# A block-sparse, LoRA-gated layer: the first LoRA factors of batch 1 loaded into the scratch buffer, and the last block product in two column halves

## Chip, core and metric

The kernel runs on one core of one Trainium2 chip. The metric is device time in microseconds (us), the median of several runs; lower is better. The kernel has five instruction streams: TensorE (PE, matmuls; its weight loads are shown as PEld), VectorE (DVE), ScalarE (ACT), GpSimd (POOL) and SyncE (SP), which does nothing here but issue DMAs. ACT and POOL issue some DMAs too.

## What is computed

```
xn = layernorm(x)                              # x: 2 batches x 1024 x 1024, over the last axis
W  = weight where its 32x32 block of mask is non-zero, else 0
s  = xn @ W.T + bias
coeffs = softmax((mean over tokens of xn) @ Wq.T @ keys.T / sqrt(128))     # 8 experts, per batch
g  = silu(xn @ W_org.T + sum_e coeffs[e] * (xn @ down[e]) @ up[e])
out = x + s * g
```

All data is fp32. There are 8 experts of rank 64, so all LoRA factors together have rank 512: with the softmax coefficients multiplied into the up factors, the gate's weight for one batch is `W_org.T + down @ (c * up)`, 1024 x 1024.

## The kernel before

Every large product is a split one: each operand is kept as a rounded high part and a low remainder, and three matmuls (high x high, high x low, low x high) are accumulated in PSUM. So TensorE does three 128x128 by 128x512 matmuls for each pair of tiles. A high part is written by ScalarE (a copy), the low part by VectorE (a subtraction).

The order of the work on TensorE, VectorE, ScalarE and GpSimd is written by hand (`manual_schedule`, L617): these engines do their instructions in the order in which the code makes them. SP is not among them. A scheduler that simulates the kernel puts SP's DMA issues in order; a DMA then waits in SP's queue until its buffer is free, and everything behind it waits too.

The stages, in order:

- Batch 0 is done as plain products, 8 token tiles by 2 column halves for s and for the gate. Each of these tiles is a `gemm` (L431): 8 contraction tiles `kt`, three matmuls each (L425 to L427), with a weight held in a "slot" of 8 tiles, high and low. `phase` (L496) runs 8 such tiles; behind each it runs some `jobs` that prepare what comes next.
- In the phase of the gate's second half (`jobs_c`, L948), job i loads and masks tile i of the weight of the s product's second half: `s_mul` (L270) loads a 128x512 tile `ws` into staging, VectorE multiplies it by the mask (L274), ScalarE writes the high part into the slot (L277), and `s_lo` writes the low part (L282). Jobs 1 to 5 also prepare sums of batch 1's inputs, which are stored to DRAM (`xv`) from GpSimd's queue (L487).
- Jobs 6 and 7 compute batch 1's softmax coefficients. `steps[1]` (`query`) multiplies the summed inputs by the query weights `wq_sb` on VectorE (L321), `steps[2]` (`scores`) runs in the middle of the last tile of the phase, and `steps[3]` (`soft`) ends in four coefficients per partition (L352).
- Then `scale_up(1, 0)` (L359) makes the scaled up factors of batch 1's first column half: four tiles of 128x512, each loaded by SP (L364), scaled and rounded by ScalarE (L367, the tile `cut`), its low part made by VectorE (L368). Behind it stands job 7's `s_mul`, in the same hand-written order.
- Next come 8 tiles of batch 0's s product (`s_tile`, L1007), with 16 `fold`s (L969) between them. Each fold loads a tile of down (`ds`) and of W_org (`wo`), splits down (`dhi`, L380, and `dlo`, L381), multiplies it by the four `cut` tiles (12 matmuls, L389 to L391), adds W_org (L396), and stores the folded weight to DRAM. Fold 7 makes the second column half's factors, `scale_up(1, 1, homes)`. Some folds are followed by a `fill` (L990), which loads a tile of `xv` into scratch (L1000) and splits it (L1001, L1002).
- Batch 1 is done with a scheme of seven block products in place of eight. There are 8 units, s and gate in turn; `quad` (L1157) does one, a 2 x 2 arrangement of output blocks 128x512, numbered (i, t) here. It runs 7 `product`s (L1143) of 12 matmuls each into three PSUM banks: `pa`, `pb` and `py`. `out_tile` (L1108) finishes a block. In the first unit of a pair it keeps a gate tile. In the second it multiplies (L1124 for s: PSUM plus bias, times the kept tile), adds the residual x and stores to `out` (L1134). In the last unit the residual comes from a tile loaded by `res_load` (L1136), three buffers of which are used in turn, and VectorE adds it (L1133).

Buffers that matter: the staging pool `stage` has 6 buffers of 128x512 (tag `st`), shared by `ws`, the `us` tiles of `scale_up`, `ds`, `wo` and the sums' tile `xt`; a tile takes the buffer that came free first. The scratch tile `misc` (L101) has three parts of 128x512. Part 0 first holds the mask's expansion matrix, parts 1 and 2 the query weights `wq_sb` (L117). Later all three serve the fills and the second `scale_up` as landing places.

The end of the last unit, before, is this:

```python
            nc.scalar.copy(pa, pb)
            nc.vector.tensor_tensor(pb, pb, s5, ALU.add)
            slot(4)
            product(u, 6, 2, py, False)
            out_tile(u, 0, 1, py)
            out_tile(u, 1, 1, pb)
            res_load(u, 1, 0)
            slot(5)
            product(u, 3, 6, pa, False)
            out_tile(u, 1, 0, pa)
```

Of the kernel before, what the change touches and what calls it, by code (L numbers as in the profile page):

```python
# [14 lines left out]
ALU = mybir.AluOpType  # L15
AX = mybir.AxisListType

P = 128
B = 2
S = 1024  # L20
D = 1024
NKT = D // P
NH = 512
NQ = 256
# [8 lines left out]
def kernel(  # L33
# [26 lines left out]
    nc = tc.nc  # L60
# [5 lines left out]
    def close(*cms):  # L66
# [34 lines left out]
    misc = c0pool.tile([P, 3, NH], F32, name="misc")  # L101
# [4 lines left out]
        out=ex4, in_=ex4, compare_op=ALU.is_ge, fill=0.0, base=0,  # L106
# [3 lines left out]
        out=ex4, in_=ex4, compare_op=ALU.is_ge, fill=0.0, base=3,  # L110
# [407 lines left out]
    J = lambda f, *a: (lambda: f(*a))  # L518
# [98 lines left out]
    with tc.manual_schedule(engines={mybir.EngineType.PE, mybir.EngineType.DVE, mybir.EngineType.Activation, mybir.EngineType.Pool}):  # L617
# [330 lines left out]
        def jobs_c(i):  # L948
            if i == 6:
                yield steps[0]  # L950
                yield steps[1]
            if i == 7:
                yield steps[3]
                yield J(scale_up, 1, 0)
            yield J(s_mul, s1, 1, i)
            yield J(s_lo, s1, 1, i)
            if i in (1, 3):
                yield J(wide_load, (i + 3) // 2, 0)
                yield J(wide_load, (i + 3) // 2, 1)
            if i < 6:  # L960
                yield J((wide_a, wide_b)[i % 2], 1 + i // 2)

        split_at[(0, 1, 7)] = steps[2]
        phase("y", 0, 1, y01, False, jobs_c)


# [20 lines left out]
        xw = {}  # L987
# [27 lines left out]
        units = [("s", 0), ("y", 0), ("y", 1), ("s", 1), ("y", 2), ("s", 2), ("y", 3), ("s", 3)]  # L1015
# [88 lines left out]
        gates = {}  # L1104
        held = {}
        pools_b1 = {}

        def out_tile(u, i, t, ps):  # L1108

            kind, p = units[u]  # L1110
            n = p + 4 * i
            bias = bias_t[:, n : n + 1]
            if u % 2 == 0:
                g = pools_b1["gate"].tile([P, NH], F32, name="gate")
                if kind == "s":
                    nc.scalar.activation(g, ps, AF.Identity, bias=bias)
                else:
                    nc.scalar.activation(g, ps, AF.Silu)
                gates[(p, i, t)] = g
                return  # L1120
            g = gates.pop((p, i, t))
            res = held.pop((i, t), None)
            if kind == "s":
                nc.vector.scalar_tensor_tensor(g, ps, bias, g, ALU.add, ALU.mult)  # L1124
            else:
                y = pools_b1["tmp"].tile([P, NH], F32, name="yt", tag="yt", bufs=1)
                nc.scalar.activation(y, ps, AF.Silu)
                nc.vector.tensor_tensor(g, g, y, ALU.mult)  # L1128
            if res is None:
                nc.gpsimd.dma_start(g, xT[n * P : (n + 1) * P, S + t * NH : S + (t + 1) * NH], accum_op=ALU.add)  # L1130
                res = g
            else:
                nc.vector.tensor_tensor(res, res, g, ALU.add)  # L1133
            nc.sync.dma_start(out[S + n * P : S + (n + 1) * P, t * NH : (t + 1) * NH], res)  # L1134

        def res_load(u, i, t):  # L1136
            if u == len(units) - 1:
                n = units[u][1] + 4 * i
                res = pools_b1["tmp"].tile([P, NH], F32, name="rest", tag="rest", bufs=3)
                nc.sync.dma_start(res, xT[n * P : (n + 1) * P, S + t * NH : S + (t + 1) * NH])  # L1140
                held[(i, t)] = res

        def product(u, a, m, ps, start, js=range(4)):  # L1143
            o = ow[u]
            for j in js:
                for k, (wl, xl) in enumerate(((0, 0), (0, 1), (1, 0))):
                    nc.tensor.matmul(  # L1147
                        ps, lhsT=o[:, a, wl, j, :], rhs=xw[j][:, m, xl, :],
                        start=start and j == 0 and k == 0, stop=j == 3 and k == 2, skip_group_check=True,
                    )  # L1150

        def snap(ps, tag):
            t = pools_b1["tmp2"].tile([P, NH], F32, name=tag, tag=tag, bufs=1)
            nc.scalar.copy(t, ps)  # L1154
            return t

        def quad(u, ahead, behind=()):  # L1157

            def after(k):
                for job in behind[k : k + 1]:  # L1160
                    for f in job:
                        f()

            def slot(k):
                for job in ahead[k]:
                    job()

            pa = ps_acc.tile([P, NH], F32, name="acc_ps", tag="acc_ps")
            if u == 0:
                py = ps_s.tile([P, NH], F32, name="py", tag="ps_s")  # L1170
                product(u, 0, 0, pa, True, (0, 1))
                product(u, 4, 3, py, True, (0, 1))
                product(u, 0, 0, pa, True, (2, 3))
            else:
                product(u, 0, 0, pa, True)
            after(0)
            pb = ps_acc.tile([P, NH], F32, name="acc_ps", tag="acc_ps")
            nc.scalar.copy(pb, pa)  # L1178
            slot(0)
            if u == 0:  # L1180
                product(u, 4, 3, py, True, (2, 3))
            else:
                py = ps_s.tile([P, NH], F32, name="py", tag="ps_s")
                product(u, 4, 3, py, True)
            after(1)
            s5 = snap(py, "s5")
            res_load(u, 0, 0)
            slot(1)
            product(u, 5, 4, pb, False)
            after(2)  # L1190
            s2 = snap(pb, "s2")
            nc.vector.tensor_tensor(py, py, s2, ALU.add)  # L1192
            res_load(u, 0, 1)
            slot(2)
            product(u, 1, 1, pa, False)
            after(3)
            out_tile(u, 0, 0, pa)
            res_load(u, 1, 1)
            slot(3)
            product(u, 2, 5, pb, False)  # L1200
            after(4)
            nc.scalar.copy(pa, pb)
            nc.vector.tensor_tensor(pb, pb, s5, ALU.add)
            slot(4)
            product(u, 6, 2, py, False)
            out_tile(u, 0, 1, py)
            out_tile(u, 1, 1, pb)
            res_load(u, 1, 0)
            slot(5)
            product(u, 3, 6, pa, False)  # L1210
            out_tile(u, 1, 0, pa)
            slot(6)
# [10 lines left out]
        behind = [[J(fill, j, m, xs_pool) for j in (2, 3)] for m in ORDER_X[2:]]  # L1223
        behind[1].insert(0, store_late)
        quad(0, ahead, behind)
        close(cm_xs)
        cm_t, pools_b1["tmp"] = open_pool("tmp", 1, side="right")
        for u in range(1, len(units)):
            quad(u, unit_jobs(u + 1))
# [57 lines left out]
```

## Time and profile before

| what | value |
|---|---|
| median of 3 runs (lowest, highest) | 461.75 us (460.07, 463.16) |
| the profiled execution | 462.08 us |
| its span, first to last instruction | 460.1 us |
| mean granted TensorE clock | 0.986 |
| DMA traffic over the span | 89.52 MB, mean 195 GB/s |

TensorE's busy time by stretch of the span, from the table by stretches:

| stretch (us) | PE busy (us) | granted clock | DMA share |
|---|---|---|---|
| 80 to 140 | 60.00 of 60 | 1.00 | 0.73 |
| 140 to 200 | 59.67 of 60 | 1.00 | 0.65 |
| 200 to 209 | 9.00 of 9 | 1.00 | 1.00 |
| 209 to 220 | 8.27 of 11 | 0.69 | 0.79 |
| 220 to 254 | 34.00 of 34 | 1.00 | 0.84 |
| 258 to 298 | 40.00 of 40 | 1.00 | 0.75 |
| 308 to 440 | 132.00 of 132 | 1.00 | 0.42 |
| 440 to 456 | 15.16 of 16 | 1.00 | 0.14 |

How to read it: a row of the profile names the source line, the engine, the operation, what it writes and reads, and its shape; then come times in us. "PE busy" counts an engine with a matmul in flight; at half the granted clock it is busy too, so the clock stands beside it. A timeline row has the start in us, the duration in us, the engine and line, and in square brackets how long the engine had been idle and what released it. "SPq" rows are DMA issues; the time on the row is that of the issue, and landing is told apart.

### The profile page before, as it was taken

How to read it: one execution, taken by the hardware profiler on the slowest of the kernel's cores; microseconds unless marked ns; L12 is line 12 of the kernel's file. 1: busy time of each engine (PE TensorE's matmuls, PEld its weight loads, DVE VectorE, ACT ScalarE, POOL GpSimd, SP SyncE). 2: the span in 40 equal slices, each digit the busy share in tenths (PEclk: the TensorE clock that was granted, in tenths of full speed). 3: DMA queues.
4: the chain of work that ended last, by engine and by line, in shares of the span. 5: the costliest groups of instructions: out<-in, count | busy, mean ns of one | idle time of the engine just before them, and what ended most of it. 6: DMA issues, size and time to landing. Idle time of an engine off the chain costs nothing.

```text
span 460.1 us, 5752 instructions
## 1 busy us (share of the span) xinstructions
PE 444.7 (97%) x2047; PEld 365.4 (79%) x2047; DVE 305.1 (66%) x492; ACT 169.3 (37%) x277; POOL 59.5 (13%) x72
## 2 busy tenths in 40 slices
PE   7799999999999999997999999999999999999995
PEld 5689888888887888885888788877888888888884
DVE  5889778666775788866546776669466294465624
ACT  3576624363323132213324233158243422441510
POOL 3764210000010202230000000000020020002000
PEclk9899999999999999997999999999999999999999
DMA  8995406687862586799778985664274246218003
GB/s 267 390 350 196 146 24 205 183 281 255 287 230 93 186 317 227 277 309 303 243 249 276 297 274 152 207 219 137 79 147 134 85 98 177 91 24 220 31 1 114
DMA packets 47404, 89.52 MB, mean 195 GB/s; under 512 B 4752, under 2 KB 14992, under 8 KB 47376
## 3 DMA queue, kind: packets, MB, share of 16 engines
q1 hardware_dynamic: 32784, 70.28, 46.1%
q0 software_dynamic: 3840, 10.49, 8.9%
q10 hardware_dynamic: 10752, 8.39, 5.7%
q8 instruction: 16, 0.26, 0.2%
q14 instruction: 12, 0.10, 0.1%
HBM read 69.21 MB, written 19.92 MB: 194 GB/s over the span
## 4 chain that ended last, share of the span: by engine, by line
PE 85%; DVE 8%; DMA 4%; issue 1%; ACT 1%; SPq 0%; ACTq 0%; DVEq 0%
PE acc_ps L1147 23%; PE acc_ps L425 11%; PE acc_ps L426 11%; PE acc_ps L427 11%; PE py L1147 9%; PE psw L391 6%; PE psw L389 6%; PE psw L390 6%; DMA ws<-in_wT_dram 2%; DMA raw<-in_x_dram 1%; DVE slot L558 1%; DVE ramp L549 1%; DMA misc<-in_up_dram 1%; DVE st L144 1%; DVE xw L1002 1%
## 5 line engine op out<-in xcount | busy, mean ns | idle before, releaser
L1147 PE MATMUL acc_ps<-xw,ow 128*128 128x512 f32 x480 | 113.6, 393 | 0.4 <-ACT acc_ps L1178 0.4
L425 PE MATMUL acc_ps<-slot,xgrp 128*128 128x512 f32 (+1 forms) x288 | 107.4, 373 | 2.8 <-ACT slot L277 2.7
L426 PE MATMUL acc_ps<-slot,xgrp 128*128 128x512 f32 (+1 forms) x288 | 106.8, 371 | 2.7 <-DVE slot L558 2.7
L427 PE MATMUL acc_ps<-slot,xgrp 128*128 128x512 f32 (+1 forms) x288 | 106.4, 369 | 0.7 <-DVE xgrp L570 0.7
L1147 PEld LDWEIGHTS acc_ps<-xw,ow 128*128 128x128 f32 x480 | 90.0, 188 | 21.3 <-ACT acc_ps L1178 0.8
L426 PEld LDWEIGHTS acc_ps<-slot,xgrp 128*128 128x128 f32 x288 | 54.9, 191 | 12.6 <-DVE slot L558 3.6
L425 PEld LDWEIGHTS acc_ps<-slot,xgrp 128*128 128x128 f32 x288 | 54.8, 190 | 12.3 <-ACT slot L277 3.1
L427 PEld LDWEIGHTS acc_ps<-slot,xgrp 128*128 128x128 f32 x288 | 55.0, 191 | 10.2 <-DVE xgrp L570 1.1
L391 PE MATMUL psw<-cut,dlo 128*128 128x512 f32 x128 | 50.9, 397 | 0.8 <-DVE dlo L381 0.8
L389 PE MATMUL psw<-cut,dhi 128*128 128x512 f32 x128 | 51.0, 399 | 0.0
L390 PE MATMUL psw<-cut,dhi 128*128 128x512 f32 x128 | 50.6, 395 | 0.0
L1147 PE MATMUL py<-xw,ow 128*128 128x512 f32 x192 | 46.9, 392 | 0.0
L1147 PEld LDWEIGHTS py<-xw,ow 128*128 128x128 f32 x192 | 36.1, 188 | 8.1
L1047 DVE TENSOR_TENSOR ow<-raw,ow 128x1024 fp32r<-128x1024 f32 (+1 forms) x32 | 34.5, 1087 | 10.4 <-ACT ow L1046 10.4
L1130 POOL DMA_DIRECT2D gate<-in_xT_dram x12 | 10.5, 906 | 203.0 <-DVE gate L1128 133.9
L380 ACT CAST dhi<-ds 128x512 fp32r<-128x512 f32 x32 | 19.8, 617 | 40.0 <-PE psw L390 23.8
L396 DVE TENSOR_TENSOR wo<-wo,psw 128x512 f32<-128x512 f32 x32 | 22.0, 686 | 18.6 <-PE psw L391 18.5
L1046 ACT CAST ow<-raw 128x1024 fp32r<-128x1024 f32 (+1 forms) x32 | 29.4, 940 | 1.6 <-DVE wo L396 1.6
L391 PEld LDWEIGHTS psw<-cut,dlo 128*128 128x128 f32 x128 | 24.5, 192 | 6.7 <-DVE dlo L381 1.2
L390 PEld LDWEIGHTS psw<-cut,dhi 128*128 128x128 f32 x128 | 24.6, 192 | 5.4
L389 PEld LDWEIGHTS psw<-cut,dhi 128*128 128x128 f32 x128 | 24.6, 192 | 5.2
L1192 DVE TENSOR_TENSOR py<-py,s 128x512 f32<-128x512 f32 x8 | 5.6, 698 | 30.7 <-ACT s L1154 30.7
(160 smaller groups left out, 477.6 us busy)
## 6 DMA issues: line engine op xcount, KB each, us to landing
ds<-in_down_dram SPq DMA_DIRECT2D x32, 256.0 KB, 3.7
wo<-in_worgT_dram SPq DMA_DIRECT2D x32, 256.0 KB, 3.8
raw<-in_x_dram SPq DMA_DIRECT2D x11, 512.0 KB, 6.5
res<-in_x_dram SPq DMA_DIRECT2D x16, 256.0 KB, 3.8
out_dram<-res ACTq DMA_DIRECT2D x16, 256.0 KB, 2.7
raw<-in_wu_dram SPq DMA_DIRECT2D x8, 512.0 KB, 5.1
yu<-wo ACTq DMA_DIRECT2D x16, 256.0 KB, 4.1
xs<-xv SPq DMA_DIRECT2D x16, 256.0 KB, 4.0
```

What stands on the lines that cost most here:

```text
L380: nc.scalar.copy(dhi, ds)
L389: nc.tensor.matmul(ps, lhsT=dhi[:, c, :], rhs=u[c][:, 0, :], start=c == 0, stop=False)
L390: nc.tensor.matmul(ps, lhsT=dhi[:, c, :], rhs=u[c][:, 1, :], start=False, stop=False)
L391: nc.tensor.matmul(ps, lhsT=dlo[:, c, :], rhs=u[c][:, 0, :], start=False, stop=c == 3)
L396: nc.vector.tensor_tensor(ws, ws, ps, ALU.add)
L425: nc.tensor.matmul(ps, lhsT=xs[:, kt, 0, cols], rhs=w[:, kt, 0, wc], start=kt == 0, stop=False)
L426: nc.tensor.matmul(ps, lhsT=xs[:, kt, 0, cols], rhs=w[:, kt, 1, wc], start=False, stop=False)
L427: nc.tensor.matmul(ps, lhsT=xs[:, kt, 1, cols], rhs=w[:, kt, 0, wc], start=False, stop=kt == NKT - 1)
L1046: nc.scalar.copy(o[:, a:b, 0], raw[:, a:b])
L1047: nc.vector.tensor_tensor(o[:, a:b, 1], raw[:, a:b], o[:, a:b, 0].bitcast(F32), ALU.subtract)
L1130: nc.gpsimd.dma_start(g, xT[n * P : (n + 1) * P, S + t * NH : S + (t + 1) * NH], accum_op=ALU.add)
L1147: nc.tensor.matmul(ps, lhsT=o[:, a, wl, j, :], rhs=xw[j][:, m, xl, :], start=start and j == 0 and k == 0, stop=j == 3 and k == 2, skip_gro ...
```

## The change

There are two edits.

The first: `scale_up(1, 0)` gets homes for three of its four tiles, the three parts of `misc`. `scale_up` uses `homes[c]` where there is one, and a staging tile only for c = 3.

The second is in the last unit alone. Block (1, 1) is finished ahead of the product `py`; the residual of block (1, 0) is loaded ahead of it too, in the code; and the last product, into `pa`, is done for columns 0 to 255 and then for columns 256 to 511, each half with its own end and its own store. For this `product` and `out_tile` get a column range.

```diff
@@ jobs_c
             if i == 7:
                 yield steps[3]
-                yield J(scale_up, 1, 0)
+                yield J(scale_up, 1, 0, [misc[:, k, :] for k in range(3)])
             yield J(s_mul, s1, 1, i)
             yield J(s_lo, s1, 1, i)
@@ out_tile
-        def out_tile(u, i, t, ps):
+        def out_tile(u, i, t, ps, cols=None):
...
+            if cols is not None:
+                g, res = gates[(p, i, t)][:, cols], held[(i, t)][:, cols]
+                nc.vector.scalar_tensor_tensor(g, ps[:, cols], bias, g, ALU.add, ALU.mult)
+                nc.vector.tensor_tensor(res, res, g, ALU.add)
+                c0 = t * NH + cols.start
+                nc.sync.dma_start(out[S + n * P : S + (n + 1) * P, c0 : c0 + NQ], res)
+                return
@@ product
-        def product(u, a, m, ps, start, js=range(4)):
+        def product(u, a, m, ps, start, js=range(4), cols=slice(0, NH)):
...
                     nc.tensor.matmul(
-                        ps, lhsT=o[:, a, wl, j, :], rhs=xw[j][:, m, xl, :],
+                        ps[:, cols], lhsT=o[:, a, wl, j, :], rhs=xw[j][:, m, xl, cols],
@@ quad
             slot(4)
+            if u == len(units) - 1:
+                out_tile(u, 1, 1, pb)
+                res_load(u, 1, 0)
+                product(u, 6, 2, py, False)
+                out_tile(u, 0, 1, py)
+                for c in (slice(0, NQ), slice(NQ, NH)):
+                    product(u, 3, 6, pa, False, cols=c)
+                    out_tile(u, 1, 0, pa, c)
+                return
             product(u, 6, 2, py, False)
             out_tile(u, 0, 1, py)
             out_tile(u, 1, 1, pb)
-            res_load(u, 1, 0)
             slot(5)
             product(u, 3, 6, pa, False)
             out_tile(u, 1, 0, pa)
```

## The prediction

> **What bounds the kernel now.** I read the page first, then the chain of waits, then the timeline of SP's queue and the table by stretches around the one place where TensorE stands still, and last the timeline of the end.
>
> ```profile
> span 460.1 us, 5752 instructions
> PE 444.7 (97%) x2047; PEld 365.4 (79%) x2047; DVE 305.1 (66%) x492; ACT 169.3 (37%) x277; POOL 59.5 (13%) x72
> PEclk9899999999999999997999999999999999999999
> ```
>
> TensorE is the bound: 97% busy, so only its gaps, its slow clock and the work behind its last matmul can be won. The clock row has one low digit in mid-kernel, slice 19 (207 to 219 us). The chain of waits, in order of time, says what happens there:
>
> ```profile
> 202.82 8.54 DMA ws<-in_wT_dram
> 211.38 0.70 DVE ws L274
> 212.11 0.63 ACT slot L277
> 212.78 0.80 PE acc_ps L425
> ```
>
> The last tile of the weight for the s half (job 7) is loaded late, takes 8.54 us to land, and then needs VectorE and ScalarE before TensorE may go on. TensorE's previous matmul started at 209.66; with 0.227 us from one 512-column matmul to the next (12 of them take 2.73 us in the chain), it has stood since 209.89. The timeline of SP's queue says why the load is late:
>
> ```profile
> 195.45 0.37 SPq L272 DMA_DIRECT2D ws<-in_wT_dram  x1
> 195.88 1.89 SPq L364 DMA_DIRECT2D us<-in_up_dram  x4
> 199.90 1.55 SPq L1000 DMA_DIRECT2D misc<-xv  x2
> 202.82 0.33 SPq L272 DMA_DIRECT2D ws<-in_wT_dram  x1
> 207.55 0.33 SPq L375 DMA_DIRECT2D ds<-in_down_dram  x1
> ```
>
> Four factor loads take four of the six staging buffers, and the ws load goes out only at 202.82, right after VectorE's last read of the previous ws tile (L282, 202.10 to 202.79): it waits for that buffer. By then the DMA engines are full (share 1.00 from 200 to 209 us), also with five stores to xv.
>
> The table by stretches (its last three columns: granted clock, DMA share, GB/s) prices the stop:
>
> ```profile
> 211.00:212.00 1.00, 0.00 (x0) 0.00 (x0) 0.62 (x1) 0.00 (x0) 0.00 (x0) 1.00 0.85 264
> 212.00:213.00 1.00, 0.22 (x1) 0.22 (x1) 0.32 (x2) 0.89 (x2) 0.00 (x0) 0.56 0.92 295
> 213.00:214.00 1.00, 1.00 (x2) 0.56 (x3) 1.00 (x2) 1.00 (x3) 0.00 (x0) 0.50 0.99 240
> ...
> 254.00:258.00 4.00, 3.22 (x15) 2.33 (x14) 4.00 (x6) 1.86 (x3) 0.00 (x0) 1.00 0.88 297
> ```
>
> About 2.2 us after TensorE stops the clock halves, and matmuls are 0.427 us apart until 219.10. From 209.89 to 219.10 fourteen steps are made, worth 14 x 0.227 = 3.18 us: the place loses 6.03 us. The last row is the only other stop of the middle, 0.8 us around 255, and there the clock stays at 1.00.
>
> **The change, part by part.** (a) *Homes of the factors.* Three of the four up tiles go to the scratch tile misc instead of staging. Nothing is added: four loads, four ScalarE copies (0.72 us), four VectorE operations (0.75 us), as before. Now the ws load needs no buffer that was just used: its staging buffer has been free since about 189 to 194 us (L282 of the earlier ws tiles). It can go out between 196 and 202 and land well before 209.7.
>
> What is late next is the chain that ran beside it. The softmax coefficients are ready at 205.98. VectorE then does:
>
> ```profile
> 206.77 2.92 DVE L368 SCALAR_TENSOR_TENSOR cut<-us,c,cut 128x512 fp32r<-128x512 f32 x4 [0.79 <-ACT cut L367]
> 211.38 0.69 DVE L274 TENSOR_TENSOR ws<-ws,m_sb 128x512 f32<-128x512 f32 x1 [1.69 <-DMA ws<-in_wT_dram]
> ```
>
> These stand ahead of the ws product on VectorE, so that starts at 209.7, not 211.38: 1.69 us sooner, no more. ScalarE's copy follows at 210.4, the first matmul at about 211.1, the second, which needs L282, at 211.8 (213.50 before): 1.7 us. If the clock is kept, the 13 steps from there to 219.10 take 2.95 us instead of 5.60: 2.65 us. Sum: 4.35 us of the 6.03.
>
> Is the clock kept? Row: a stop of 2.9 us halved it after 2.2 us, one of 0.8 us did not; the new stop is 1.2 us and a wait of 0.5 us behind it. The Trainium skill (TensorE: Matmul & The Clock Gate, Part 1 and the table "Why this matters for your kernels") lets the clock be judged in free-running windows of about 3.4 us and tells one to avoid gaps above about 3 us. By that limit the old stop of 2.9 us should hardly have dropped it, and (a) would be worth 1.7 us only; the trace shows that it dropped. I go by the rows: the new stop is nearer to 0.8, so no drop.
>
> (b) *The loads of misc.* The first factor's home (misc 0) was last read by the mask matmuls at 125 us: its load can go any time before 200. The homes of the second and third hold the query weights, read until 199.87 and 200.48 (L321), so those two loads cannot go before 199.9 and 200.5. ScalarE wants them at 206.7 and 207.4. Nearest rows, issue to landing, in this crowd:
>
> ```profile
> us<-in_up_dram SPq DMA_DIRECT2D x4, 256.0 KB, 6.5
> ...
> misc<-xv SPq DMA_DIRECT2D x2, 256.0 KB, 8.6
> ```
>
> With 6.5 us the third lands at 207.0, in time; with the 9.2 us of the second misc load it lands near 210. The 8.6 comes from standing behind four us loads in one queue, at most two of which now stand there, if SP does not put the fold's loads in between. I take 6.5, cost 0, and keep up to +1.2 us for the other end (rival 1).
>
> The three fills that used to fetch xv into misc at 161.6, 199.9 and 201.1 must now follow the factors' reads, at 207.5 to 209, and be there when ScalarE first wants one (220.69, about 216 after the gain). Landing after about 5 us is 214: hidden by the folds' matmuls. Without that cover ScalarE's in-order queue would hold the next dhi copy, which has some 2 us to spare. The fold's own ds and wo loads come earlier or equal (buffers freed by three); cost 0, as they were hidden even at 207.55. SP's order is not written by hand (the other four engines' is), so all its later waits can shift too; the one stop that depends on it, at 255, is worth 0.8 us: -0.8 to some +4 at worst, taken as 0.
>
> (c) *The end.* Before:
>
> ```profile
> 452.28 2.88 PE L1147 MATMUL acc_ps<-xw,ow 128*128 128x512 f32 x12
> 455.26 0.74 DVE L1124 SCALAR_TENSOR_TENSOR gate<-acc_ps,bias_t,gate 128x512 f32<-128x512 f32 x1
> 456.04 0.69 DVE L1133 TENSOR_TENSOR rest<-rest,gate 128x512 f32<-128x512 f32 x1
> ...
> 46.59 0.28 PE L426 MATMUL acc_ps<-slot,xgrp 128*128 128x256 f32 x1
> 46.71 0.28 PE L427 MATMUL acc_ps<-slot,xgrp 128*128 128x256 f32 x1
> ```
>
> VectorE's last operation ends at 456.73 and the store lands 2.0 us after issue. Matmuls of 256 columns are 0.12 us apart, so two halves take 24 x 0.12 = 2.88 for 2.72: +0.16. Block (1,1) moves to 451.1 to 452.55, beside the twelve py matmuls; block (0,1) runs 452.6 to 454.05; the first half's VectorE pair (0.47 and 0.41 us, scaled from 0.415 for a 256-column read of PSUM at L439) starts at 454.07. If the second half's matmuls run on meanwhile, they end at 455.4 and VectorE is done at 456.3: 0.45 sooner, and the store of half the bytes saves 0.34 more (half of 0.67 us of data at 390 GB/s): -0.8. Against this speaks a rule of the Trainium skill (PSUM — Partial Sum Buffer, "PSUM bank collisions raise a hardware error"): TensorE must not write a bank while VectorE reads it, other columns of it included, so accesses are to be guarded by bank. Both halves lie in one bank of 512 fp32. Then the second half starts when the first half's read ends, at 454.55, takes 12 x 0.12 and 0.3 to drain, VectorE ends at 457.15: 0.42 later, less 0.34: +0.1. No row of the trace shows such a pair. I take +0.1 by the rule, and keep -0.8. The earlier load of (1,0) costs nothing: SP issues it at 450.57 already, when its buffer comes free, and it lands at 453.6.
>
> Sum: -4.35 + 0.1 = -4.25 us. The profiled execution took 462.08 us (span 460.1 and 2.0 around it), 0.3 above the median of 461.75; from the median I forecast 457.5.
>
> **The rivals.** *Rival 1, slower: the scratch loads become the wait.* If SP sends us, ws, ds and wo first, the two bound loads stand where the two misc loads stood and land at 207.9 and 210.3. ScalarE and VectorE then finish the fourth factor at 212.5, the ws product starts at 212.6 and TensorE resumes near 214: about 1.2 us worse than now, clock lost as before, 463.0. It decides by when the third factor lands: each us past 207.4 costs one, and from 209.1 on the change loses (landing + 2.3 = 211.4). For it: the DMA share of 1.00 from 200 to 209 and the 8.6 row. Against: two fewer loads need stand ahead.
>
> *Rival 2: the clock drops all the same.* The stop shortens but the window still counts as idle; then some 15 matmuls run at half speed: 3.4 us lost, gain 1 us, about 460.8. The 0.8 us row speaks against it.
>
> *Rival 3: SP's new order hurts later,* at the second set of factors (240 to 256 us), where SP already waits 4.3 us for a buffer behind VectorE's factor operation. Some 4 us of stop and a lost clock (2.65) against the 4.25 gained: +2.4, 464; with the first place not won either, up to 468.
>
> **How the numbers follow.** A measurement of this kernel tells about 1%, 4.6 us, from no change: below 457.1 is faster, above 466.4 slower. My forecast: 0.58, own range 455.6 to 458.8; its centre is 0.4 us short of the 1% line, and the stop at 255 or an end without the bank guard carry it over: 0.32 faster, 0.26 same. Rival 1: 0.15, 462 to 465, with what follows it: 0.13 same, 0.02 slower. Rival 2: 0.10, 0.09 same, 0.01 faster. Rival 3: 0.17, 464 to 468: 0.05 same, 0.12 slower. Together faster 0.33, same 0.53, slower 0.14. The range 455.6 to 464.0 leaves out most of rival 3 and the edges of the others.
>
> **What would show it.** Right: the ws load of job 7 issued before 202 us, a stop of 1 to 1.3 us ended by ScalarE's L277 behind the four factor operations, clock 1.00 in that stretch, TensorE's work after it some 4.3 us earlier, and the last half's matmuls starting after VectorE's first-half read. Wrong: factor operations waiting for a DMA into misc; clock below 0.9 around 212; a new stop of several us between 216 and 300; a last half that starts without waiting.

## The result, and the profile after

The changed kernel took 462.55 us in the median of 14 runs (460.11 to 465.04). The kernel before took 461.56 us in 14 runs beside them (459.02 to 463.16). The ratio is 1.0026, with a 95% interval of 1.0002 to 1.0050: some 1.2 us slower, and inside the 1% that the prediction called no change. The forecast was 457.5 us. Rival 1 of the prediction, at 463.0 us, came nearest, and its chain of events is what the profile shows.

The profiled execution took 463.65 us. Its page, first part and clock row:

```profile
span 461.9 us, 5776 instructions
PE 444.8 (96%) x2059; PEld 366.1 (79%) x2059; DVE 305.2 (66%) x494; ACT 169.5 (37%) x277; POOL 59.3 (13%) x72
PEclk9899999999999999997999999999999999999999
```

The low clock digit is still there, in slice 19 as before. What TensorE waited for, from the view of its waits (line, releaser and its line: us in total, times, longest us), names the stop and one new wait:

```profile
PE acc_ps L425 <- ACT slot L277: 4.0, 1, 4.0
PE acc_ps L1154 <- DVE gate L1123: 0.6, 1, 0.6
```

The first was 2.7 us in the same view before. (This view counts from the modelled end of the last matmul, so it gives 0.16 us less than the prediction's count of the same stop.) SP's queue in the changed kernel, by start and duration, shows the first edit doing what it should:

```profile
196.84 0.37 SPq L272 DMA_DIRECT2D ws<-in_wT_dram  x1
197.30 0.38 SPq L375 DMA_DIRECT2D ds<-in_down_dram  x1
199.87 0.33 SPq L364 DMA_DIRECT2D misc<-in_up_dram  x1
200.29 0.89 SPq L377 DMA_DIRECT2D wo<-in_worgT_dram  x1
201.27 1.38 SPq L364 DMA_DIRECT2D misc<-in_up_dram  x1
```

The last ws load goes out at 196.84 in place of 202.82. But the second and third factor, bound to the scratch tile, go out at 199.87 and 201.27, and ScalarE then waits for them. Its timeline (in brackets: how long it had stood and for what), and VectorE's behind it:

```profile
206.28 0.72 ACT L367 ACTIVATE cut<-misc,c 128x512 fp32r<-128x512 f32 x1 [3.36 <-DVE c L352]
207.63 0.72 ACT L367 ACTIVATE cut<-misc,c 128x512 fp32r<-128x512 f32 x1 [0.63 <-DMA misc<-in_up_dram]
210.53 0.72 ACT L367 ACTIVATE cut<-misc,c 128x512 fp32r<-128x512 f32 x1 [2.17 <-DMA misc<-in_up_dram]
...
211.28 0.75 DVE L368 SCALAR_TENSOR_TENSOR cut<-misc,c,cut 128x512 fp32r<-128x512 f32 x1 [2.15 <-ACT cut L367]
211.95 0.74 DVE L368 SCALAR_TENSOR_TENSOR cut<-us,c,cut 128x512 fp32r<-128x512 f32 x1
212.62 0.68 DVE L274 TENSOR_TENSOR ws<-ws,m_sb 128x512 f32<-128x512 f32 x1
```

The three lines of ScalarE are the first three factors; waits of factor operations for a DMA into `misc` were the prediction's own first sign of being wrong. From issue to landing the second took 7.66 us and the third 9.2. So the ws product, whose data had long landed, stands on VectorE behind factors that are late: it starts at 212.62, where it started at 211.38 before. TensorE resumes at 214.00 instead of 212.78. That is 1.22 us of loss, at the clock of before (granted clock 0.70 in 209 to 220 us, 0.69 before):

```profile
209.00:220.00 11.00, 7.00 (x18) 4.92 (x17) 6.12 (x10) 3.56 (x6) 0.00 (x0) 0.70 0.76 240
```

(The columns are those of the prediction's table by stretches; the last three are granted clock, DMA share and GB/s.) The end of the changed kernel, from the timeline:

```profile
453.95 1.59 PE L1154 MATMUL acc_ps<-xw,ow 128*128 128x256 f32 x12
455.58 0.48 DVE L1123 SCALAR_TENSOR_TENSOR gate<-acc_ps,bias_t,gate 128x256 f32<-128x256 f32 x1
456.10 0.42 DVE L1124 TENSOR_TENSOR rest<-rest,gate 128x256 f32<-128x256 f32 x1
456.12 1.69 PE L1154 MATMUL acc_ps<-xw,ow 128*128 128x256 f32 x12 [0.58 <-DVE gate L1123]
457.85 0.48 DVE L1123 SCALAR_TENSOR_TENSOR gate<-acc_ps,bias_t,gate 128x256 f32<-128x256 f32 x1 [1.32 <-PE acc_ps L1154]
458.36 0.42 DVE L1124 TENSOR_TENSOR rest<-rest,gate 128x256 f32<-128x256 f32 x1
```

The second half waits 0.58 us for VectorE's read of the first. From the first matmul of the last product to VectorE's last end it is 4.83 us (4.45 before); from there to the end of the span it is 3.12 us (3.37 before). The end costs 0.38 - 0.25 = 0.13 us. With the 1.22 us of the stop that is 1.35 us. The profiled spans differ by 1.8 us; of the remaining 0.45 us, 0.34 lies in batch 1's products, where no single wait accounts for it.

That 1.35 us is near the 1.2 us of the medians is in part chance. The interval only just leaves out no change, and the stop varies from one execution to the next: it was 3.0 to 4.0 us in the four profiles of kernels with three homes, and 2.2 to 3.1 us in the three with the factors in staging and the old order (table in experiment 6). What is sure is that the forecast gain is not there.

### The profile page after: what moved, and what is told of

It is laid out like the page before. It is cut to its first block, busy times and chain, and to the rows that moved or that the text cites. A ratio compares the mean times of both kernels' runs of the same rounds, so it can differ in the third digit from the quotient of the medians.

```text
span 461.9 us, 5776 instructions
## 1 busy us (share of the span) xinstructions
PE 444.8 (96%) x2059; PEld 366.1 (79%) x2059; DVE 305.2 (66%) x494; ACT 169.5 (37%) x277; POOL 59.3 (13%) x72
## 4 chain that ended last, share of the span: by engine, by line
PE 76%; DVE 11%; DMA 8%; ACT 2%; issue 2%; SPq 0%; DVEq 0%; ACTq 0%
PE acc_ps L1154 22%; PE py L1154 9%; PE acc_ps L425 8%; PE acc_ps L426 8%; PE acc_ps L427 8%; PE psw L391 6%; PE psw L389 6%; PE psw L390 6%; DMA misc<-in_up_dram 2%; DMA ws<-in_wT_dram 2%; DMA xs<-xv 2%; DMA raw<-in_x_dram 1%; DVE slot L558 1%; DMA ds<-in_down_dram 1%; ACT slot L277 1%
## 5 line engine op out<-in xcount | busy, mean ns | idle before, releaser
L1154 PE MATMUL acc_ps<-xw,ow 128*128 128x512 f32 (+1 forms) x492 | 114.2, 388 | 1.2 <-DVE gate L1123 0.6
L425 PE MATMUL acc_ps<-slot,xgrp 128*128 128x512 f32 (+1 forms) x288 | 107.6, 374 | 4.1 <-ACT slot L277 4.0
L425 PEld LDWEIGHTS acc_ps<-slot,xgrp 128*128 128x128 f32 x288 | 54.9, 191 | 13.5 <-ACT slot L277 4.4
L381 DVE TENSOR_TENSOR dlo<-ds,dhi 128x512 fp32r<-128x512 f32 x32 | 21.9, 685 | 8.0 <-ACT dhi L380 7.9
```

The source lines that it names most:

```text
L381: nc.vector.tensor_tensor(dlo, ds, dhi.bitcast(F32), ALU.subtract)
L425: nc.tensor.matmul(ps, lhsT=xs[:, kt, 0, cols], rhs=w[:, kt, 0, wc], start=kt == 0, stop=False)
L1154: nc.tensor.matmul(ps[:, cols], lhsT=o[:, a, wl, j, :], rhs=xw[j][:, m, xl, cols], start=start and j == 0 and k == 0, stop=j == 3 and k == ...
```

## The experiments

Below, the "middle" is the time from the second scores matmul (L332) to the first block product of batch 1 (L1147 before), in the profiled execution; it leaves out what happens earlier. "Stop" is the wait of TensorE at L425 in the view of waits.

**1. Each edit alone.** The kernel before with the three homes only:

```diff
-                yield J(scale_up, 1, 0)
+                yield J(scale_up, 1, 0, [misc[:, k, :] for k in range(3)])
```

> The kernel before, with the first edit only (three parts of the scratch tile as homes; the end as before). Theory S (the second and third factor cannot be loaded before the query has read its weights, land near 207.5 and 210.5 us, and hold the factor operations, so TensorE's stop grows from 2.9 to about 4.1 us with the clock lost as before): 1.0 to 1.5 us slower than before, about 462.8. Rival E (the loss comes from the end: the second half waits for the bank and SP has one store more): no difference from before, 461.6.

Measured: 461.20 us in 22 runs, ratio 1.0004 (0.9985 to 1.0024). The waits and the stretch around them:

```profile
PE acc_ps L425 <- ACT slot L277: 3.0, 1, 3.0
...
209.00:220.00 11.00, 8.76 (x37) 7.05 (x38) 8.38 (x14) 4.72 (x8) 0.00 (x0) 1.00 0.87 279
```

The two bound loads landed 7.8 and 8.7 us after issue, and the stop is not shorter than before: the edit alone gains nothing. The loss of 1.0 to 1.5 us that was expected does not show either; the interval runs from 0.7 us faster to 1.1 us slower. In this execution the clock stayed at 1.00 through a stop of 3.0 us, which I come back to.

The changed kernel with the first edit taken back:

```diff
-                yield J(scale_up, 1, 0, [misc[:, k, :] for k in range(3)])
+                yield J(scale_up, 1, 0)
```

> The kernel before, with the second edit only (block (1,1) ahead of py, the last product in two column halves; the factors as before). Theory S: the end costs about 0.1 us, from the first matmul of the last product to the end, so no difference that can be measured. Rival E: the whole 1 us, 462.6.

Measured: 460.45 us in 14 runs, ratio 0.9990 (0.9969 to 1.0011); stop 3.1 us, and again 0.6 us between the halves. No difference can be told from it. The two ratios multiply to 0.9994 where both edits gave 1.0026; the intervals are too wide to say whether the edits disturb each other.

**2. One home only.** Only the first factor, whose place has been free since 125 us, goes to the scratch tile; the two that must wait for the query weights stay in staging.

```diff
-                yield J(scale_up, 1, 0)
+                yield J(scale_up, 1, 0, [misc[:, 0, :]])
```

> The kernel before with one scratch home only: the first factor goes to part 0, which nothing reads after 125 us; the second, third and fourth stay in staging. Theory S: the ws load of job 7 still gets an old staging buffer and goes out near 197 to 198 us, no factor waits for the query weights, TensorE's stop is about 1.2 us (209.9 to 211.1), the clock stays at 1.00, and the kernel is 4 to 4.5 us faster than before, about 457.3. Rival C (the clock halves for a stop of 1.2 us too): 1 to 2 us faster, with the granted clock near 0.5 from about 212. Rival D (in this crowd any load lands late, the ws load too): the stop stays above 2.5 us, within 1 us of before.

Measured: 459.47 us in 22 runs, ratio 0.9968 (0.9950 to 0.9986), 1.5 us gained. The profile shows what the prediction described for the whole edit:

```profile
197.37 0.38 SPq L272 DMA_DIRECT2D ws<-in_wT_dram  x1
...
PE acc_ps L425 <- ACT slot L277: 1.0, 1, 1.0
...
209.00:220.00 11.00, 9.73 (x42) 7.51 (x41) 8.34 (x14) 5.03 (x9) 0.00 (x0) 1.00 0.90 301
```

The last ws load goes out at 197.37, the stop is 1.0 us, the clock is full, and the middle is 93.2 us in place of 97.4. The mechanism is right: one freed staging buffer is enough, and the other two homes undo it. The median moved by 1.5 us, not the 4 to 4.5 expected, and not the 4.1 by which the two middles differ. Experiment 6 returns to this.

**3. Two homes**, as the dose between (the diff is that of experiment 1 with range(2)).

> Before with two scratch homes (the first and the second): the dose between one home and three. Only one factor, not two, now waits for the query weights' last read. Theory (the stop follows the landing of the last factor that is bound to the scratch tile): that load goes out about 1 us sooner than the third did and lands 1 to 1.5 us sooner; the stop at L425 is 1.5 to 2.5 us, between the 1.0 of one home and the 3.0 of three, and the median lies between 459.5 and 461.2. Rival (any bound load costs the full stop): 3 us or more, 461.

Measured: 459.19 us in 22 runs, ratio 0.9974 (0.9953 to 0.9994). The bound load went out at 201.36 and took 7.6 us; the stop was 1.7 us, ended by ScalarE's L277 as in the others. The stop stands between 1.0 and 3.0 as the theory has it; the median can't be told from that of one home.

**4. Why the bound loads take 8 to 9 us.** The prediction put the slow landing of such loads down to standing behind others in SP's queue. The other candidate is the crowd: from 199.0 to 201.3 us (in the changed kernel) GpSimd's queue issues the stores of the last group of block sums to xv, 1.75 MB. This kernel is the changed one without these five stores; the later fills of that group read the group before, so part of the output comes from other data.

```diff
+            if j == 3:
+                return
             sum_stores.append((xv[j, :, 0:2, :], ac))
...
-nc.sync.dma_start(st, xv[j, :, XV[m], :])
+nc.sync.dma_start(st, xv[min(j, 2), :, XV[m], :])
```

> The changed kernel without the five stores of the last group of sums (1.75 MB to DRAM at 199 to 209 us); the last group's loads read the group before it instead, so that part of the result is of other data. Theory S with the crowd as the cause of the 7.7 and 9.2 us: the second and third factor, issued at 199.9 and 201.3 as before, land within 4 us, near 204 and 205.5, the stop is about 1.2 us and the span some 5 us shorter than that of the changed kernel. Rival Q (the delay is the queue of SP's own loads ahead of them): landing stays at 7 us or more, and the stop above 3 us.

Measured: 457.49 us in one run, middle 93.6 us. The bound loads landed 2.7 and 4.1 us after issue, although SP's order around them is the same (a wo load between the two, a ds load behind):

```profile
198.38 0.33 SPq L364 DMA_DIRECT2D misc<-in_up_dram  x1
198.80 0.38 SPq L377 DMA_DIRECT2D wo<-in_worgT_dram  x1
199.28 0.38 SPq L364 DMA_DIRECT2D misc<-in_up_dram  x1
199.71 0.42 SPq L375 DMA_DIRECT2D ds<-in_down_dram  x1
```

From the view of DMA issues in 196 to 210 us (KB each, median us to landing), first without the stores, then in the changed kernel:

```profile
misc<-in_up_dram SPq DMA_DIRECT2D x2, 256.0 KB, 3.4
```

```profile
q1 hardware_dynamic: 1396, 2.82, 60.9%
q0 software_dynamic: 528, 1.84, 33.8%
...
xv<-bd POOLq DMA_DIRECT2D x1, 512.0 KB, 7.7
misc<-in_up_dram SPq DMA_DIRECT2D x2, 256.0 KB, 8.4
xv<-tt POOLq DMA_DIRECT2D x2, 256.0 KB, 8.2
xv<-xt POOLq DMA_DIRECT2D x1, 256.0 KB, 8.8
```

In the changed kernel the stores hold a third of the 16 DMA engines' time in this stretch, and what either queue issued between 199.6 and 203.1 us took 7.7 to 9.2 us to land. Without them the three factors run on ScalarE without a pause:

```profile
204.49 1.95 ACT L367 ACTIVATE cut<-misc,c 128x512 fp32r<-128x512 f32 x3 [3.36 <-DVE c L352]
```

So the stores make the difference of some 5 us. The place in SP's queue counts too, but alike in both: the ds load issued ahead of the second factor landed 3.1 us after that factor's issue in the changed kernel and 2.1 us after it here. From there the factor took another 4.6 us beside the stores, and 0.6 us without them. The Trainium skill (DMA: Bandwidth & Descriptors, "Queues, rings and completion order") has each DMA engine take turns between the queues that it serves, packet by packet; that fits, though no run here tests the turn itself.

**5. Another order instead of another home.** Job 7's ws load and product are emitted ahead of the coefficients and the factors; no home at all, then with the one home.

```diff
             if i == 7:
+                yield J(s_mul, s1, 1, i)
+                yield J(s_lo, s1, 1, i)
                 yield steps[3]
                 yield J(scale_up, 1, 0)
-            yield J(s_mul, s1, 1, i)
-            yield J(s_lo, s1, 1, i)
+            else:
+                yield J(s_mul, s1, 1, i)
+                yield J(s_lo, s1, 1, i)
```

> The order alone: before with job 7's ws load and product emitted ahead of the up loads and the factor operations, no scratch home. Theory (the stop of before is the buffer for the ws load, taken by the four up loads): with ws ahead it has the first free buffer and the late one is an up load, which TensorE needs later; ws issued before 198, stop at L425 under 1 us, middle interval 93 to 95 us, median 458 to 460. Rival (some other load of the crowd is then late, and what waits for it stops TensorE): a stop of 1 us or more at another line of the middle, median 460 to 462.

> Before with one scratch home, and job 7's s_mul and s_lo emitted ahead of the softmax coefficients and the factor operations, so that on VectorE and ScalarE the ws product no longer stands behind them. Theory (what is left of the stop with one home is the order on VectorE): ws lands near 204 as with one home, the ws product runs then, the stop of 1.0 us at L425 goes to 0.2 us or less, the granted clock never drops in the middle in any execution, and the middle interval (second scores matmul to batch 1's first block product) is 92 to 93 us, about 5 us shorter than before; median 456 to 459. Rival (the factors are wanted by TensorE soon after, so the stop only moves from L425 to the folds): a stop of about 1 us appears at a later line before 230 us, and the median is that of one home, 459.5.

Measured: the order alone 459.45 us (22 runs), ratio 0.9953 (0.9934 to 0.9972); with one home 459.59 us (22 runs), ratio 0.9956 (0.9937 to 0.9975). The wait at L425 is gone from both, and a wait at the first fold takes its place. The order alone:

```profile
PE psw L389 <- ACT dhi L380: 2.1, 1, 2.1
...
196.52 0.84 SPq L272 DMA_DIRECT2D ws<-in_wT_dram  x2
197.47 1.37 SPq L364 DMA_DIRECT2D us<-in_up_dram  x3
200.61 1.33 SPq L1003 DMA_DIRECT2D misc<-xv  x2
203.53 0.33 SPq L364 DMA_DIRECT2D us<-in_up_dram  x1
206.04 0.33 SPq L375 DMA_DIRECT2D ds<-in_down_dram  x1
```

Now the fourth factor and the fold's ds load wait for a staging buffer. TensorE stands for the high part of ds, which ScalarE makes at 212.94, right behind the fourth factor (landed at 212.22); ds itself landed at 212.74. With one home only ds is late, and the wait is 1.9 us. Both middles are 95.0 us, at full clock. The rival, that the stop only moves, held in the place of the stop; in time the order still gains some 2 us, without any home, and the home adds nothing to it. The 456 to 459 us expected with one home and this order were not reached.

**6. The same kernels a second time.** One pair of profiles had shown 4.1 us where the median gained 1.5. So three kernels were profiled again, unaltered.

> The kernel before unaltered, a second look at its trace. Theory: stop of 2.7 to 3.1 us at L425 behind the ws load. Whether the clock drops in the middle in every execution is open: if it does, the granted clock is 0.70 in 209 to 220 us again; if it is a matter of the execution, it may be 1.00 and the middle interval 94 us in place of 97.4.

> Before with the first scratch home alone, unaltered, a second look. Theory: a stop of 0.9 to 1.3 us at L425 and the clock at 1.00 in 209 to 220 us, middle interval 93 to 94 us. Rival (a stop of 1 us also drops the clock in a part of the executions, which would explain that its median gained 1.5 us where its profile showed 4.2): granted clock below 0.9 in that stretch.

> The changed kernel unaltered, a second look at its trace. Theory: the second and third factor land 7 to 9.5 us after issue again, the stop at L425 is 3.3 to 4.2 us, with a wait of 0.58 us between the last two halves. If the clock's drop at the stop is a matter of the execution, this one may keep it or lose it; the stop itself stays.

Measured, before again (458.08 us):

```profile
PE acc_ps L425 <- ACT slot L277: 2.2, 1, 2.2
...
209.00:220.00 11.00, 9.78 (x36) 7.72 (x37) 7.32 (x12) 4.72 (x8) 0.00 (x0) 0.84 0.82 264
```

The kernel before does not always pay what its first profile showed. Here the ws load landed after 7.5 us and not 8.54, the stop was 2.2 us, and the clock was at half speed for some 3.4 us, half as long as in the first profile ((1 - 0.84) x 11 = 1.8 us lost, against 3.4). The middle is 94.8 us, 2.5 less than in the first profile of the same kernel. The two profiles may come from different chips, but executions differ on one chip too: 27 timed runs of before on the chip of the second had mean granted clocks from 0.982 to 1.000. One home again (459.82 us): stop 0.9 us, clock 1.00 again, middle 94.6. So the second profiles of the two kernels differ by 0.2 us only. One home's middle is 1.4 us longer than in its first profile, about half of that by a longer stop later on:

```profile
253.47 0.50 PE L391 MATMUL psw<-cut,dlo 128*128 128x512 f32 x1 [1.55 <-DVE dlo L381]
```

That is the stop that the prediction gave 0.8 us at 255. It waits for 0.78 us in the first profile of before, for nothing in its second, and for 0.87 and 1.55 us with one home. The changed kernel again (462.97 us): the second and third factor landed 7.2 and 8.9 us after issue, stop 3.6 us, clock 0.69, middle 97.6, and 0.6 us between the halves.

All profiles of the study side by side:

| kernel | longest wait at 205 to 214 us | clock in 209 to 220 us | middle, us |
|---|---|---|---|
| before | 2.7 | 0.69 | 97.4 |
| before, again | 2.2 | 0.84 | 94.8 |
| second edit alone | 3.1 | 0.69 | 96.7 |
| changed | 4.0 | 0.70 | 98.7 |
| changed, again | 3.6 | 0.69 | 97.6 |
| changed, two banks (experiment 7) | 3.3 | 0.69 | 98.6 |
| first edit alone | 3.0 | 1.00 | 95.7 |
| two homes | 1.7 | 0.84 | 96.5 |
| order alone | 2.1 | 1.00 | 95.0 |
| one home, ws first | 1.9 | 1.00 | 95.0 |
| one home | 1.0 | 1.00 | 93.2 |
| one home, again | 0.9 | 1.00 | 94.6 |
| changed, no last stores | 0.8 | 1.00 | 93.6 |
| all that worked (experiment 7) | 0.6 | 1.00 | 93.5 |

**7. The wait between the halves, and all that worked together.** The last product's halves in two accumulators, hence two banks of PSUM; and that end joined with one home and ws first.

```diff
+            if u == len(units) - 1:
+                pc = ps_acc.tile([P, NH], F32, name="acc_ps", tag="acc_ps")
+                halves = ((pa, slice(0, NQ)), (pc, slice(NQ, NH)))
+                for h, c in halves:
+                    nc.scalar.copy(h[:, c], pb[:, c])
...
-                for c in (slice(0, NQ), slice(NQ, NH)):
-                    product(u, 3, 6, pa, False, cols=c)
-                    out_tile(u, 1, 0, pa, c)
+                for h, c in halves:
+                    product(u, 3, 6, h, False, cols=c)
+                    out_tile(u, 1, 0, h, c)
```

> The changed kernel with the two column halves of the last product in two banks of PSUM (one more acc_ps tile, ScalarE copies each half into its own). Theory (the 0.58 us wait between the halves is VectorE's read of the same bank): the second half's first matmul follows the first half's last one without a wait, and from the first matmul of the last product to the end of VectorE's last operation it takes 4.2 to 4.3 us in place of 4.83; the end comes 0.5 to 0.6 us sooner than in the changed kernel, median 461.9 to 462.1. Rival (the second half waits for VectorE by the order of the queue, whichever bank it is in): still a wait of 0.5 us ended by VectorE's L1123, 4.8 us.

> All that has worked: one scratch home, job 7's ws load and product ahead of the factor operations, the last product in two halves in two banks of PSUM. If the gains add: the middle as with one home and ws first (5 us shorter than before in an execution of before that lost the clock there), the end 0.5 us sooner than before; median 455.5 to 458.5. If executions that lose the clock elsewhere (the ramp at 10 to 30 us, 230 to 254 us) carry the rest, the median stays at 458.5 to 459.

Measured, two banks: 460.76 us in 14 runs, ratio 0.9978 (0.9953 to 1.0003). The timeline of its end:

```profile
452.55 3.03 PE L1154 MATMUL acc_ps<-xw,ow 128*128 128x256 f32 x24
454.21 0.48 DVE L1123 SCALAR_TENSOR_TENSOR gate<-acc_ps,bias_t,gate 128x256 f32<-128x256 f32 x1
...
456.13 0.42 DVE L1124 TENSOR_TENSOR rest<-rest,gate 128x256 f32<-128x256 f32 x1
```

All 24 matmuls run as one group, without a wait, and from their start to VectorE's last end it is 4.00 us instead of 4.83. So the wait came from the shared accumulator, not from the order of the queue. (Each accumulator tile fills one bank, so this run cannot tell bank from tile.) The gain at the end is 0.83 us, more than the 0.5 to 0.6 expected: the wait of 0.58 us is counted from the modelled end of the last matmul, while without a wait the next one starts 0.12 us after the last one's start. From the first half's start to the second's it took 2.17 us with the wait and 1.43 without. The median against before is not clear of no change. All together: 458.75 us in 22 runs, ratio 0.9945 (0.9923 to 0.9967), faster than before by some 2.5 us and the lowest median ratio of the study; its interval overlaps that of the order alone. The 455.5 to 458.5 us given for gains that add in full were just missed.

## Why the prediction was wrong

*The first edit's mechanism (a): right, and undone by another step.* The ws load left early, as said. With one home the stop becomes what the prediction worked out: TensorE had stood 1.2 us when it resumed, and the clock stayed at 1.00 in both profiles.

*The loads of `misc` (b): the step that failed.* The prediction took 6.5 us for them, the row of the four us loads, and cost 0; it put the 8.6 us of the misc fills down to their place behind four other loads. They took 7.66 and 9.2 us, TensorE's stop grew from 2.7 to 4.0 us instead of shrinking, and experiment 4 shows that the stores to xv made the difference: without them the loads took 2.7 and 4.1 us and the stop was 0.8 us. The fills had been the nearer row: same queue, same moment, while the four us loads went out 2.5 to 5.4 us earlier, all before the first of these stores (198.60 us in before). The break-even given, a third factor landing at 209.1, was passed at 210.5. Rival 1's chain came out as written: ws product at 212.6 (212.62), TensorE at 214 (214.00), 463.0 us (462.55). It had been given a chance of 0.15.

*The price of the clock (a): too high.* 2.65 us was read from one execution in which the clock lost two stretches of some 3.4 us. The second profile of before lost one. Over the timed runs beside the experiments, the mean granted clock was 0.990 or less in 75 of 145 runs of before, in 13 of 22 with three homes, in 4 of 22 with two, in 5 of 22 with one, in 3 of 22 with the order alone; and in 11 of 14 of the changed kernel in the runs of the result. The five profiles with such a mean each had three half-speed stretches of some 3.4 us ahead of the last matmul, but in that of two homes two of the three fell at the start. So the counts fit a clock that a shorter stop protects, and a kernel before that pays for it only in part of its executions. Together with the longer stop near 253 us, that can turn the 4.1 us between two profiles into 1.5 in the median. How the runs split between these causes is not shown, since a timed run has no trace.

*The stop at 255 (b) and rival 3.* Cost 0 held in the first profile of the changed kernel (0.82 us against 0.78 before), but not over all of them. The stop was 0.43 to 1.48 us in the four profiles with three homes, 1.0 on average, and 0.78, 0 and 0 us in the three with the factors in staging and the old order. With two homes and with the order alone it was 1.54. So it tends to grow with the change and takes part of the gain; why was not followed up. The four us of rival 3 appeared nowhere.

*The fills from xv (b): right.* Issued from 207.81 behind the factors, the three landed after 2.6 to 4.0 us, by 214.7; ScalarE first wanted one at 221.97. (In before the third was issued at 200.51, not at 201.1; nothing rests on it.)

*The end (c): right.* +0.1 was forecast, +0.13 measured; 0.42 us for the guard, 0.38 measured. The Trainium skill's rule (PSUM — Partial Sum Buffer, "PSUM bank collisions raise a hardware error"), to guard PSUM by bank and not by column, gave the right forecast: TensorE waited for a read of other columns of its bank. With two banks the end took 4.00 us, 0.45 less than before, which is what the prediction gave for VectorE's end without the guard.

## What to carry to other kernels

When a load is given a new home, ask when that home is last read and what the DMA engines carry at that moment; cost it by the slowest row of the same queue in the same microseconds, and if that row crosses your own break-even point, it is the forecast and not the tail. Move only the loads whose new home has long been free: here one of three did the work, and emitting the urgent load first did as well without any home. A slow-clock loss read from one profile is one throw of a die: take several profiles before giving it a price.

## What the runs showed of the hardware

- The length of a stop does not settle whether the clock drops. It was halved after waits of 1.7 and 2.2 us, for some 3.4 us each time, and after five of 2.7 to 4.0 us for twice as long; but it stayed at 1.00 through waits of 1.9, 2.1 and 3.0 us. At 1.0 us and less it never dropped (four profiles), nor at the later stops near 253 us, up to 1.55 us. With two homes it dropped 0.9 us after TensorE had resumed. Windows that run free of the program, as the Trainium skill describes them (TensorE: Matmul & The Clock Gate, Part 1), would give such a scatter. Its advice to avoid gaps above some 3 us (same page, "Why this matters for your kernels") is too generous by the row of 1.7.
- The same program can also lose 2 us at the start: in the first profile of before the granted clock in 10 to 30 us was 0.91 and the second scores matmul came at 202.2 us; in the second it was 1.00 and 200.1 us.
- Loads of 256 KB landed 7.66 and 9.2 us after issue beside 1.75 MB of GpSimd's stores (6.5 to 9.2 in the four profiles with three homes), and 2.7 and 4.1 us after issue without them.
